# Sparse attention with residual and layer norm: three more output products in the last stretch, and additions moved behind the last tile

## The chip, the cores and the metric

The kernel runs on one core of a Trainium2 chip. The metric is device time in microseconds (us) of one execution, and the comparison is between medians of several executions. The engines are named as in the profile: PE (TensorE, with PEld for its weight loads), DVE (VectorE), ACT (ScalarE), POOL (GpSimd) and SP (SyncE, which here only issues DMAs).

## What is computed

There are 16 batches of 1024 nodes with 512 features, one 0/1 adjacency matrix for all of them, and 8 heads of 64. Each batch goes through masked attention, an output projection, the residual and a layer norm:

```python
q = (x @ Wq + bq).reshape(b, n, H, HD)
k = (x @ Wk + bk).reshape(b, n, H, HD)
v = (x @ Wv + bv).reshape(b, n, H, HD)
scores = jnp.einsum('bqhd,bkhd->bhqk', q, k) / jnp.sqrt(jnp.float32(HD))
scores = scores + (1.0 - adj)[None, None, :, :] * -1000000000.0
attn = jax.nn.softmax(scores, axis=-1)
out = jnp.einsum('bhqk,bkhd->bqhd', attn, v).reshape(b, n, d)
return out @ Wo + bo
# and around it:
x = _layernorm(x + _L0_gnn_ref(x, adj, ...), axis=-1)
```

The adjacency matrix is sparse: its first nodes have many neighbours and most have few.

## The kernel before

**Tiles.** The nodes are sorted by their number of neighbours, and the sorted order is cut into eight tiles of 128 queries. Tile `t` of batch `b` has the number `8 * b + t`. For a tile the kernel gathers one key and value row for each query and step, with an indirect DMA on POOL (L1260, tile `kvg`), so attention is a list of 530 steps, called *places*: a batch has 32 or 34 of them (batch 15, the last, has 34). A place multiplies queries and keys (DVE L1281), reduces by head (DVE L1285), exponentiates (ACT L1296), weighs the values (ACT L1309 or DVE L1313) and adds them up (DVE L1325, or PE L1334 and L1335 for steps whose rows belong to other tiles). When a tile is closed, `normalise` divides (DVE L1346 to L1355), PE transposes the result (L1369, `poT`), ACT copies it (L1373, `oT`).

**Fronts.** Beside attention, PE computes the projections of later batches (L748, L790 for q, L947 for keys and values in the seven-product form of Strassen). They are a list of units, `fronts`, worked off at a pace that is set at the start of each batch from what is left and from what the batch's own output products and sums will take. `fronts` is planned to be empty twelve places before batch 15 starts, 46 places before the end of attention. From there on is the last stretch.

**Output products.** `finish` multiplies a closed tile's `oT` by Wo on PE (L790, `po`). In the last stretch the bias is added by a small PE product (L1078), earlier by DVE. After attention's end `finish` adds the bias to y on DVE ahead of the product (L1067). `complete` then adds the residual y (DVE L1099 where the bias is added by DVE, and L1100), squares (ACT L1107), takes the power of the variance (POOL L1113, or L1143 for two tiles at once), shifts (DVE L1116), normalises (ACT L1121) and stores rows with an indirect DMA on POOL (L1125).

**The order of work.** The whole program is one loop over places, and each engine's instructions run in the order in which the loop emits them. `now[0]` is the place, `total` is 530. `later(k, fn)` puts a piece of work `k` places ahead (list `plan`), `later_last` puts it behind that place's weighing (list `rest`). Within a place come exponentials, products, gathers, weighing, adds, scores, then `normalise` of the tile closed one place before, then `plan`, then `rest`, then PE's units as far as a credit reaches. In the last stretch the credit grows by 3.4 a place (`LAST_SHARE`); an output product costs 4 x 0.86, about one place. No product may begin in the two places before the end:

```python
if (
    not finishing and len(done) > (LAZY if fronts else 0) and n > loaded.get(done[0], n) + 1
    and n > last_finish + bool(fronts) and not total - 2 <= n < total
):
```

**Spilled tiles.** Tiles whose number is in `SPILL` (20 of them: tiles 3 and 6 of batches 4 to 11, and 102, 103, 106, 107) aren't multiplied in their own batch. Their `oT` is written to DRAM by SP, and so is their x (`STORED`, tensor `residual`), two places before the x buffer is filled again. In the last stretch `reload` brings one of them back every second place: `oT` by SP (L1055, into the three buffers `e`, `w`, `g` that the fronts used) and y by SP (L1026) from `residual`, where a tile that isn't spilled has y gathered by POOL (L1029). PSUM tiles of these products rotate among four buffers with the tag `fill`.

Of the kernel before, what the change touches and what calls it, by code (L numbers as in the profile page):

```python
# [41 lines left out]

LAZY = 2

SPILL = (*(8 * b + t for b in range(4, 12) for t in (3, 6)), 102, 103, 106, 107)
STORED = {*SPILL, *(i for i in range(102, 128) if i % 8 > 1)}
LATE = 12

# [129 lines left out]
def kernel(  # L178
# [75 lines left out]
    with ExitStack() as main:  # L254
# [85 lines left out]
        def tiles_of(b):  # L340
            return [t for t in range(NT) if t or b < PAIRED_FROM or merged(b)]

        def number(b, t):
            return b * NT + t if t < NT else -1
# [3 lines left out]
        x_rows = x.rearrange("b n d -> (b n) d")  # L348
        spill = {i: dram.tile([P, D], F32, name=f"spill_{i}") for i in SPILL}
        residual = {i: dram.tile([P, D], F32, name=f"residual_{i}") for i in sorted(STORED)}  # L350
# [89 lines left out]
        now, plan, rest, urgent, known, waiting, combined = [0], {}, {}, [], [], [], []  # L440

        def later(k, fn):
            plan.setdefault(now[0] + k, []).append(fn)

        def later_last(k, fn):
            rest.setdefault(now[0] + k, []).append(fn)
# [337 lines left out]
        def product(name, lhs, w, out):  # L784

            def unit(c):
                if c == 0:
                    PS[name] = fill_psum(name)
                p = PS[name]
                nc.tensor.matmul(p, lhs(c), w[:, c, :], start=(c == 0), stop=(c == NPAIR - 1))  # L790
                if c == NPAIR - 1:
                    del PS[name]
                    later(1, lambda: out(p))

            return [(PRODUCT, lambda c=c: unit(c), None) for c in range(NPAIR)]
# [210 lines left out]
        def rows_of(b, t):  # L1006

            if t == LONE_TILE or t == 0 and merged(b):
                n, col, base = (2 * SPARED, NT + 2, b - 1) if t else (P, NT + 1, b - 1)
            elif t == MORE_TILE:  # L1010
                n, col, base = (LONE - SPARED) * (B - PAIRED_FROM), NT + 3, 0
            else:
                n, col, base = P, NT if t == ONE_KEY and b >= PAIRED_FROM else t, b
            return n, asked_row[0:n, col:col + 1], base * N * D
# [30 lines left out]
        def keep_mean(b, p):  # L1045

            m = work.tile([1, D], F32, tag="q", name=f"out_mean_{b}", bufs=2)
            nc.scalar.copy(m, p[0:1, :])
            nc.sync.dma_start(mean_rows[b:b + 1, :], m)
            if merged(b):  # L1050
                later(2, lambda: lone_tiles.append(b))
# [7 lines left out]
        def finish(b, t):  # L1059


            mean_row = t == ONE_KEY and b >= PAIRED_FROM
            plain = bool(fronts) or mean_row
            biased = not plain and now[0] < total

            if now[0] >= total and not plain:
                nc.vector.tensor_tensor(Y[b, t], Y[b, t], bo_bc, op=OP.add)  # L1067

            def out(p):
                OT.pop((b, t))  # L1070
                if mean_row:
                    keep_mean(b, p)
                complete(b, t, p, plain)

            units = product(f"po_{b}_{t}", lambda c: OT[b, t][:, ts(c, P)], W["o"], out)
            if biased:
                def bias():
                    nc.tensor.matmul(  # L1078
                        PS[f"po_{b}_{t}"], three.to_broadcast([P, P]), bo_3, start=False, stop=False
                    )  # L1080

                units.insert(2, (BIAS, bias, None))
            return units

        def complete(b, t, p, plain):
            n, rows, offset = rows_of(b, t)
            y, p = Y[b, t][0:n, :], p[0:n, :]
            single = fronts or now[0] > total + 3 or n < P
            if single:
                st = small.tile([P, 5], F32, name="stats", bufs=6)[0:n, :]  # L1090
            else:

                second = bool(half)
                if not second:
                    half.append([small.tile([P, 2, 5], F32, name="stats_2", bufs=5)])
                st2 = half[0][0]
                st = st2[:, int(second), :]
            if plain:
                nc.vector.tensor_tensor(y, p, y, op=OP.add)  # L1099
            nc.vector.scalar_tensor_tensor(  # L1100
                y, bo_bc[0:n, :] if plain else p, 1.0, y, op0=OP.mult, op1=OP.add, accum_out=st[:, 0:1]
            )

            def spread():

                sq = work.tile([P, D], F32, tag="ysq", name=f"ysq_{b}_{t}", bufs=1)
                nc.scalar.activation(sq[0:n, :], y, AF.Square, bias=st[:, 0:1], scale=-float(D), accum_out=st[:, 2:3])  # L1107

            def variance():
                nc.vector.tensor_scalar(st[:, 2:3], st[:, 2:3], 1.0 / D ** 3, EPS, op0=OP.mult, op1=OP.add)  # L1110

            def power():
                nc.gpsimd.tensor_tensor(st[:, 3:4], st[:, 2:3], neg_half[0:n, :], op=OP.pow)  # L1113

            def shift():
                nc.vector.scalar_tensor_tensor(  # L1116
                    st[:, 4:5], st[:, 0:1], -1.0 / D, st[:, 3:4], op0=OP.mult, op1=OP.mult
                )

            def norm_out():  # L1120
                nc.scalar.activation(y, y, AF.Identity, bias=st[:, 4:5], scale=st[:, 3:4])  # L1121
                later(2, store)

            def store():
                nc.gpsimd.indirect_dma_start(  # L1125
                    out=out_rows[b, t], out_offset=bass.IndirectOffsetOnAxis(ap=rows, axis=0),
                    in_=y, in_offset=None, element_offset=offset,
                )
                del Y[b, t]

            later_last(1, spread)
            if single:
                late = 1 if fronts else 0
                later(2 + late, variance)
                later(3 + late, power)
                later(4 + 2 * late, shift)
                later_last(5 + 2 * late, norm_out)
            elif second:
                later(3, variance)
                mate_shift, mate_norm_out = half.pop()[1]  # L1140

                def powers():
                    nc.gpsimd.tensor_tensor(  # L1143
                        st2[:, :, 3:4], st2[:, :, 2:3], neg_half[:, :, None].to_broadcast([P, 2, 1]), op=OP.pow
                    )

                def shifts():
                    mate_shift()
                    shift()

                later(4, powers)
                later(6, shifts)
                later_last(6, mate_norm_out)
                later_last(7, norm_out)
            else:
                later(3, variance)
                mine = half[0]
                mine.append((shift, norm_out))

                def alone():  # L1160
                    if half and half[0] is mine:
                        half.pop()
                        power()
                        later(2, shift)
                        later_last(3, norm_out)

                later(6, alone)
# [197 lines left out]
        def turn(b, t, o):  # L1365
            def transpose():
# [4 lines left out]
                def out():  # L1371
                    OT[b, t] = work.tile([P, D], F32, tag="oT", name=f"oT_{b}_{t}", bufs=LAZY + 2)
                    nc.scalar.copy(OT[b, t], p)  # L1373
                    if number(b, t) in SPILL:
                        later(1, lambda: nc.sync.dma_start(spill[b * NT + t], OT.pop((b, t))))
# [74 lines left out]
        done, coming, spilled, gathered, fronts, guarded = [], [], [], [0], [], []  # L1450

        total = len(blocks)

        def kept_y():
            return sum(t == "mean" or number(b, t) not in SPILL for b, t in Y)

# [24 lines left out]
        with tc.manual_schedule():  # L1481
# [9 lines left out]
            def needed(b, part):  # L1491
                b += int(part)
                if b >= B:
                    return fronts_time
                return fronts_by[b - 1] + (part - int(part)) * (fronts_by[b] - fronts_by[b - 1])
# [7 lines left out]
            while n < total or plan or rest or urgent or done or finishing or spilled or lone_tiles or not guarded:  # L1503
# [6 lines left out]
                elif n in start:  # L1510

                    b = start.index(n)
                    left = sum(u[0] for u in fronts)
                    ahead = EARLY + FIRST * (1 - max(0, b - 1) / LATE)
                    goal = fronts_time - needed(b + 2, ahead / NBT)
                    kept = sum(number(b, t) not in SPILL for t in tiles_of(b))
                    share = (max(0.0, left - goal) + kept * NPAIR * PRODUCT + NS * SUM) / (start[b + 1] - start[b])
# [105 lines left out]
```

## Time and profile before

| | |
|---|---|
| median of 5 runs | 1900.1 us (1887.47 to 1903.67) |
| the profiled execution, its own time | 1901.09 us |
| its span, first to last instruction | 1899.2 us |
| mean granted TensorE clock | 0.986 |
| spilled tiles brought back (`oTs<-spill`) | 20, issued from 1713.2 to 1846.2 us |
| indirect stores of rows (`out_dram<-y`, L1125) | 129 |
| gathers of y (L1029) on POOL, and loads of y by SP (L1026) | 93 and 36 |
| output products on PE (L790, `po`) | 816 records with `oT`, 160 with a reloaded `oTs` |

The profile is of one execution; its own time is 1.0 us above the median of the runs. Two records of L790 stand for one matmul of 128 x 128 by 128 x 512, so an output product has eight. Times of the timeline are us from the span's start. "[4.15 <-PE po L790]" behind an instruction says that its engine was idle for 4.15 us ahead of it, and who released it.

### The profile page before, as it was taken

To read this page: it belongs to the slowest core of one execution; us is meant where nothing else is said; L and a number is where in the kernel's file an instruction comes from. 1 tells how busy PE (TensorE), PEld (TensorE's weight loads), DVE (VectorE), ACT (ScalarE), POOL (GpSimd) and SP (SyncE) were. 2 spreads that over 40 slices of the span, in tenths; PEclk is the share of its full clock that TensorE was granted. 3 is DMA by queue.
4 is the path that set the end of the run, shared out by engine and by line. 5 is a ranking of instruction groups with operands and counts; after the bars stand their busy time and mean duration, and the time that the engine had idled before them with its cause. 6 is when DMAs were issued, how large, how long until landed. Compare 5 with 4: busy or idle time off the path is not lost.

```text
span 1899.2 us, 25241 instructions
## 1 busy us (share of the span) xinstructions
PE 1816.8 (96%) x5136; PEld 878.8 (46%) x5150; DVE 1687.1 (89%) x3462; ACT 1565.8 (82%) x6184; POOL 1268.6 (67%) x1189
## 2 busy tenths in 40 slices
PE   7969899999999999999999999999999999999995
PEld 3424444444444444444444445444444444444442
DVE  6878689999998999999899999999899999997784
ACT  3626768988888898999889898999799988987785
POOL 1355665776675777767676776777677776665783
PEclk9989999999999999999999999999999999999998
DMA  7355677898888889998898988998999999898992
GB/s 279 116 171 178 203 254 266 282 326 290 307 287 282 288 309 327 305 319 304 292 315 297 331 290 305 325 308 310 301 321 314 322 338 320 297 331 307 343 315 100
DMA packets 188150, 544.64 MB, mean 287 GB/s; under 512 B 32602, under 2 KB 32622, under 8 KB 187986
## 3 DMA queue, kind: packets, MB, share of 16 engines
q0 software_dynamic: 116400, 382.82, 61.0%
q1 hardware_dynamic: 68510, 154.30, 21.8%
q10 hardware_dynamic: 3076, 5.82, 0.9%
q14 instruction: 121, 0.99, 0.2%
q8 instruction: 43, 0.70, 0.1%
HBM read 419.52 MB, written 144.34 MB: 297 GB/s over the span
## 4 chain that ended last, share of the span: by engine, by line
PE 71%; DVE 12%; ACT 6%; issue 3%; DMA 2%; another core or an unknown queue 1%; POOL 1%; SPq 0%; DVEq 0%; POOLq 0%; ACTq 0%
PE po L790 18%; PE pq L790 14%; PE pp L947 12%; PE x L947 9%; PE z L947 9%; ACT pv L1309 3%; PE pxT L748 3%; PE poT L1369 2%; DVE qk L1281 2%; DVE s L1285 2%; PE sum L1335 2%; PE sum L1334 2%; DVE pv L1325 1%; ACT sq_k L800 1%
## 5 line engine op out<-in xcount | busy, mean ns | idle before, releaser
L1309 ACT ACTIVATE pv<-kvg,pv 128x64 f32<-128x64 f32 x3600 | 908.2, 342 | 2.2 <-issue 2.1
L1260 POOL DMA_INDIRECT kvg<-kv_pair,place_row x462 | 528.2, 1143 | 263.1 <-issue 89.4
L790 PE MATMUL po<-wo,oT 128*128 128x512 f32 x816 | 375.7, 598 | 0.9 <-ACT oT L1373 0.5
L790 PE MATMUL pq<-wq,xT 128*128 128x512 f32 x792 | 369.0, 597 | 2.9 <-DVE q L821 2.4
L1285 DVE TENSOR_REDUCE s<-qk 128x8 f32<-128x512 f32 x530 | 360.5, 680 | 6.7
L1281 DVE TENSOR_TENSOR qk<-qt,kvg 128x512 f32<-128x512 f32 x434 | 296.5, 683 | 0.8 <-DMA kvg<-kv_pair,place_row 0.8
L947 PE MATMUL x<-b,xT 128*128 128x512 f32 x504 | 238.8, 596 | 1.1 <-issue 1.0
L947 PE MATMUL pp<-t,s 128*128 128x512 f32 x504 | 237.2, 593 | 1.5 <-ACT sq_k L800 1.5
L790 PEld LDWEIGHTS po<-wo,oT 128*128 128x128 f32 x816 | 154.5, 192 | 177.0 <-issue 166.5
L1325 DVE TENSOR_TENSOR pv<-pv,pv 128x520 f32<-128x520 f32 x329 | 228.5, 694 | 4.0 <-ACT pv L1309 3.0
L790 PEld LDWEIGHTS pq<-wq,xT 128*128 128x128 f32 x792 | 148.0, 191 | 167.6 <-issue 153.8
L1001 POOL DMA_INDIRECT x<-in_x_dram,asked_row x120 | 132.0, 1100 | 77.0 <-PE pxT L748 32.0
L1125 POOL DMA_INDIRECT out_dram<-y,asked_row x129 | 147.2, 1141 | 40.7 <-issue 25.1
L1296 ACT ACTIVATE pv<-s,absent 128x8 f32<-128x8 f32 x434 | 127.2, 295 | 53.3 <-DVE s L1285 38.8
L800 ACT ACTIVATE sq_k<-kv 128x128 bf16<-128x128 f32 x512 | 151.0, 302 | 8.5 <-DVE kv L970 4.0
L947 PEld LDWEIGHTS x<-b,xT 128*128 128x128 f32 x504 | 94.8, 192 | 109.5 <-issue 103.2
L947 PEld LDWEIGHTS pp<-t,s 128*128 128x128 f32 x504 | 94.1, 190 | 109.3 <-issue 101.6
L1214 POOL DMA_INDIRECT qg<-q_rows,query_row x96 | 109.0, 1135 | 33.4 <-issue 25.9
L947 PE MATMUL z<-b,s 128*128 128x512 f32 x252 | 120.6, 601 | 4.7 <-DVE kv L975 4.4
L1029 POOL DMA_INDIRECT y<-in_x_dram,asked_row x93 | 100.3, 1078 | 36.0 <-issue 27.4
L947 PE MATMUL z<-t,s 128*128 128x512 f32 x252 | 119.6, 597 | 0.0
L947 PE MATMUL pp<-t,xT 128*128 128x512 f32 x252 | 118.5, 593 | 0.6 <-ACT oT L1373 0.6
(276 smaller groups left out, 2746.7 us busy)
## 6 DMA issues: line engine op xcount, KB each, us to landing
kv_pair<-kv SPq DMA_DIRECT2D x98, 512.0 KB
q_rows<-q SPq DMA_DIRECT2D x106, 256.0 KB
qt<-q_rows SPq DMA_DIRECT2D x98, 256.0 KB
residual<-x SPq DMA_DIRECT2D x36, 256.0 KB
y<-residual SPq DMA_DIRECT2D x36, 256.0 KB
kv_rows<-kv SPq DMA_DIRECT2D x15, 512.0 KB
kvg<-kv_pair,place_row POOLq DMA_INDIRECT x462
kv_pair<-kv SPq DMA_DIRECT2D x28, 256.0 KB
```

What stands on the lines that cost most here:

```text
L790: nc.tensor.matmul(p, lhs(c), w[:, c, :], start=(c == 0), stop=(c == NPAIR - 1))
L800: nc.scalar.activation(sq, s[:, ts(h, P)], AF.Square, scale=scale, accum_out=sums[:, h:h + 1])
L947: nc.tensor.matmul(R[bank], l[:, ts(c, P)], right[:, c, :], start=(first and c == 0), stop=(c == 1), skip_group_check=True,)
L1001: nc.gpsimd.indirect_dma_start(out=y, out_offset=None, in_=x_rows, in_offset=bass.IndirectOffsetOnAxis(ap=asked_row[:, t:t + 1], axis=0), ...
L1125: nc.gpsimd.indirect_dma_start(out=out_rows[b, t], out_offset=bass.IndirectOffsetOnAxis(ap=rows, axis=0), in_=y, in_offset=None, element_o ...
L1214: nc.gpsimd.indirect_dma_start(out=q, out_offset=None, in_=q_rows[b % ROWS], in_offset=bass.IndirectOffsetOnAxis(ap=rows, axis=0))
L1260: nc.gpsimd.indirect_dma_start(out=KG[n], out_offset=None, in_=rows, in_offset=bass.IndirectOffsetOnAxis(ap=(place_row if b else key_row)[ ...
L1281: nc.vector.tensor_tensor(QK[n], q, KG[n][:, 0:D], op=OP.mult)
L1285: nc.vector.tensor_reduce(S[n], QK.pop(n).rearrange("p (h d) -> p h d", d=HD), axis=AX.X, op=OP.add)
L1296: nc.scalar.activation(PV[n][:, D:], S.pop(n), AF.Exp, bias=bias)
L1309: nc.scalar.activation(pv[:, ts(h, HD)], v[:, ds(D + h * HD, HD)], AF.Copy, scale=pv[:, D + h:D + h + 1])
L1325: nc.vector.tensor_tensor(PV[b, t], PV[b, t], pv, op=OP.add)
```

## The change

Tiles 45, 69 and 93 (tile 5 of batches 5, 8 and 11) join the spilled ones, which are then 23. And where the last stretch is on and an output product's `out` comes up in one of attention's last three places (`total - 3` to `total - 1`), its `complete` is put off to place `total`. There it stands in `plan`, behind the last tile's `normalise`. The PSUM tile is held until then.

```diff
-SPILL = (*(8 * b + t for b in range(4, 12) for t in (3, 6)), 102, 103, 106, 107)
+SPILL = (*(8 * b + t for b in range(4, 12) for t in (3, 6)), 45, 69, 93, 102, 103, 106, 107)
 STORED = {*SPILL, *(i for i in range(102, 128) if i % 8 > 1)}
...
                 if mean_row:
                     keep_mean(b, p)
-                complete(b, t, p, plain)
+                if not fronts and total - 4 < now[0] < total:
+                    later(total - now[0], lambda: complete(b, t, p, plain))
+                else:
+                    complete(b, t, p, plain)
```

## The prediction

> **What bounds the kernel now.** I read the page first, then the windows of single batches, then the chain of waits inside two of them, and last the timeline of the final 45 us.
>
> ```profile
> span 1899.2 us, 25241 instructions
> PE 1816.8 (96%) x5136; PEld 878.8 (46%) x5150; DVE 1687.1 (89%) x3462; ACT 1565.8 (82%) x6184; POOL 1268.6 (67%) x1189
> PE 71%; DVE 12%; ACT 6%; issue 3%; DMA 2%; another core or an unknown queue 1%; POOL 1%; SPq 0%; DVEq 0%; POOLq 0%; ACTq 0%
> ```
>
> PE carries 71% of the chain that ended last, but 96% of busy PE is an average over unlike stages. So I cut the span at the first place of batches 5, 8, 11 and 13 (one L1285 reduction a place, counted off in the timeline) and added the last stretch, from the end of batch 14 until PE first runs dry. The columns are length, then busy time and count of PE, PEld, DVE, ACT, POOL, then granted clock, DMA share and GB/s.
>
> ```profile
> 728.50:833.20 104.70, 104.63 (x305) 51.38 (x305) 99.30 (x195) 95.85 (x397) 73.76 (x68) 1.00 0.93 313
> 1041.30:1143.20 101.90, 101.17 (x292) 49.52 (x291) 97.19 (x190) 91.71 (x369) 74.79 (x69) 1.00 0.93 316
> 1348.30:1451.90 103.60, 101.72 (x296) 49.63 (x296) 99.14 (x194) 94.02 (x391) 72.35 (x63) 1.00 0.90 310
> 1553.30:1649.00 95.70, 90.54 (x260) 44.16 (x260) 92.92 (x178) 88.29 (x374) 61.25 (x55) 0.98 0.91 315
> 1764.40:1861.60 97.20, 93.64 (x257) 44.22 (x260) 79.24 (x220) 76.69 (x245) 73.06 (x68) 0.98 0.89 311
> ```
>
> The first three rows are the batches that lose a product (tiles 45, 69 and 93 are tile 5 of batches 5, 8 and 11). PE is idle there for 0.07, 0.73 and 1.88 us; DVE is second, 3 to 5 us behind. In batch 13 DVE leads, and the time is 2.8 us above its 92.92. The chain, asked for batches 8 and 11 alone, says the same:
>
> ```profile
> by line: PE pq L790 21.9%; PE pp L947 21.0%; PE po L790 17.3%; PE x L947 13.5%; PE z L947 11.8%; PE pxT L748 4.7%; PE poT L1369 3.0%; PE sum L1335 2.6%; PE sum L1334 2.5%; PE pm L858 1.0%; DVE g L966 0.7%; issue 0.5%
> by line: PE po L790 19.8%; PE pq L790 16.5%; PE pp L947 14.8%; PE z L947 11.6%; PE x L947 8.3%; issue 3.3%; DVE qk L1281 2.9%; PE pxT L748 2.9%; PE poT L1369 2.7%; DVE s L1285 2.6%; ACT pv L1309 1.9%; PE sum L1335 1.7%; PE sum L1334 1.7%; D
> ```
>
> So a product removed from these batches should shorten them by about its PE time. The end looks different: after 1861.6 PE waits.
>
> ```profile
> 1861.60:1864.35 2.75, 0.00 (x0) 0.00 (x1) 2.68 (x9) 2.75 (x12) 0.00 (x0) 1.00 0.24 98
> 1864.35:1867.75 3.40, 0.66 (x4) 0.42 (x4) 3.40 (x11) 1.97 (x7) 3.05 (x3) 0.86 0.00 0
> 1867.75:1871.00 3.25, 3.22 (x6) 2.19 (x7) 1.46 (x6) 3.25 (x12) 1.47 (x3) 0.50 0.42 161
> 1880.10:1884.00 3.90, 3.90 (x5) 1.63 (x6) 1.03 (x4) 0.65 (x1) 2.56 (x3) 0.56 0.36 128
> ```
>
> PE has nothing to do for 2.75 us, then does 0.66 us in 3.40 while DVE is full, and then works at half clock. This is where products put off from the middle can go.
>
> **The change, part by part: what leaves the three batches.** The duration rows are three of the timeline and four groups of batch 8 (count, busy us, mean ns):
>
> ```profile
> 1842.31 1.88 PE L790 MATMUL po<-wo,oTs 128*128 128x512 f32 x4
> 1844.03 0.38 PE L1078 MATMUL po<-bo,three 128*128 128x512 bf16 x1
> 1845.96 0.59 PE L1334 MATMUL sum<-pv,sums 128*128 128x256 f32 x2
> L1099 DVE TENSOR_TENSOR y<-po,y 128x512 f32<-128x512 f32 x6 | 4.1, 681 | 0.0
> L1100 DVE SCALAR_TENSOR_TENSOR y<-bo_bc,y 128x512 f32<-128x512 f32 x6 | 4.2, 702 | 0.2
> L1107 ACT ACTIVATE ysq<-y,stats 128x512 f32<-128x512 f32 x5 | 3.6, 712 | 0.0
> L1121 ACT ACTIVATE y<-y,stats 128x512 f32<-128x512 f32 x6 | 4.8, 804 | 0.0
> L1125 POOL DMA_INDIRECT out_dram<-y,asked_row x7 | 7.5, 1072 | 2.0 <-issue 1.4 <-ACT oT L1373 0.3 <-ACT e L960 0.3
> ```
>
> From 1842.31 to 1845.96 PE does one biased product: 3.65 us. The row of four has (1.88 - 0.59) / 3 = 0.43 us from start to start; a product is eight such records, 3.44 us, so the bias is the other 0.21. In the middle a product has no bias row: each moved tile takes 3.44 us from PE there, 0.68 + 0.70 = 1.38 us from DVE, 0.71 + 0.80 = 1.5 us from ACT, and from POOL a store (1.07) and the gather of y. What comes in are two direct writes of 256 KB on SP's queue (oT to spill, x to residual); what goes out is a gather and a store of 256 KB each, so the batch's DMA bytes stay the same. SP's later transfers (the queries and the keys' rows) stand behind these writes, and the gather of the next x tile, which goes two places later, waits in POOL's queue until the residual write has left the buffer. Both have several places in hand; I take 0.7 us for all of it, between 0 and 5.1 us (3 x 512 KB at the 310 GB/s of batch 11).
>
> After the loss PE holds 101.2, 97.7 and 98.3 us in the three batches. DVE holds 97.9, 95.8 and 97.8; with batch 13's 2.8 us on top it reaches 100.7, 98.6 and 100.6. The later of the two is late next: 101.2, 98.6 and 100.6, which is 3.4 (PE's 3.44), 3.3 and 3.0 us less than now. That is 9.7 of the 10.3 us that leave PE; less the 0.7 I take **-9.0 us**. The lower end of the gain is 0 (second rival), the upper 13.3 (first rival).
>
> **Where the products go.** Count places from attention's end, so that -1 is the last of its 530. One spilled tile is loaded every second place, number k at place -46 + 2k. Before, number 19 is the last: loaded at -8, multiplied at -6, added at -5. Now number 20 is loaded at -6 and multiplied at -4; number 21, loaded at -4, falls due at -2, where no product may begin, and goes to 0; number 22 goes to +1. Of the natural tiles, (15, 7) is multiplied at -3 and (15, 6), the last, is transposed at +1 and multiplied at +3. The additions due at -3 (number 20) and at -2 (tile (15, 7)) now stand at place 0, behind the last tile's normalising. Those due at -5 and before are untouched. The rows of the end as it is:
>
> ```profile
> 1869.65 3.62 PE L790 MATMUL po<-wo,oT 128*128 128x512 f32 x4
> 1871.03 2.01 ACT L1309 ACTIVATE pv<-kvg,pv 128x64 f32<-128x64 f32 x8
> 1873.49 1.94 PE L790 MATMUL po<-wo,oT 128*128 128x512 f32 x4
> 1875.46 0.69 DVE L1100 SCALAR_TENSOR_TENSOR y<-po,y 128x512 f32<-128x512 f32 x1 [4.15 <-PE po L790]
> 1876.08 0.70 DVE L1325 TENSOR_TENSOR pv<-pv,pv 128x520 f32<-128x520 f32 x1
> 1877.72 0.69 DVE L1355 TENSOR_TENSOR o<-o,rden 128x512 f32<-128x512 f32 x1
> 1878.46 0.66 PE L1369 MATMUL poT<-ident,o 128*128 128x128 f32 x4 [3.04 <-DVE o L1355]
> 1880.09 5.40 PE L790 MATMUL po<-wo,oT 128*128 128x512 f32 x8 [0.19 <-ACT oT L1373]
> 1885.52 0.69 DVE L1100 SCALAR_TENSOR_TENSOR y<-po,y 128x512 f32<-128x512 f32 x1 [4.32 <-PE po L790]
> 1888.18 1.04 POOL L1125 DMA_INDIRECT out_dram<-y,asked_row  x1 [0.20 <-issue]
> 1889.52 0.96 POOL L1125 DMA_INDIRECT out_dram<-y,asked_row  x1 [0.30 <-issue]
> ```
>
> *The wait that goes.* DVE stands 4.15 us for the product of (15, 7), with the last tile's last add (1876.08) queued behind. That add needs only ACT's weighing, which ends at 1873.04. Without the addition in front it runs 3.0 us earlier, and the last tile's o is ready at 1878.4 - 3.0 = 1875.4.
>
> *What PE does instead.* Number 20 starts behind the transposes at 1865.0 and ends at 1868.65; the sums (0.9) follow to 1869.6, (15, 7) with bias to 1873.25 (now at full clock), number 21 without bias to 1876.7. Only then comes the last transpose, until 1877.4; number 22 ends at 1880.85, with oT's copy under it, and the last product at 1884.4, against 1885.5 before. It counts 3.44 us and not the 5.40 of the row at clock 0.56, since PE has not been idle ahead of it. So PE takes three more products and still ends 1.1 us sooner: they fill 2.8 us of idleness, the lost half clock, and the wait of 3.0 us ahead of 1878.46.
>
> The Trainium skill ("TensorE: Matmul & The Clock Gate", Part 1) says that the clock halves after an idle window of about 3.4 us and that the windows run freely. By that, the gap at 1861.6 may still cost half a window, an estimated 1.7 us more at the end; the trace has both outcomes (1.00 in the gap, 0.50 soon after), so it does not fix which.
>
> *What is late next.* Stores. The shifts of the two put-off tiles stand at place +6, those of 21 and 22 at +8, all behind the last tile's addition (+4) on DVE; their normalising lies on ACT behind the last tile's squares, and their stores on POOL ahead of the last store. Before, one store (1888.18) stood there. From one store to the next POOL takes 1.34 us (1889.52 - 1888.18), so five instead of two add 3 x 1.34 = 4.0 us. **Tail: -1.1 + 4.0 = +2.9 us.** If the stores hid, it would be -1.1; the far end is the third rival.
>
> *Cover of the loads.* The three reloads must land before PE comes to them.
>
> ```profile
> 1846.16 0.32 SPq L1055 DMA_DIRECT2D oTs<-spill  x1
> 1846.52 11.04 SPq L1026 DMA_DIRECT2D y<-residual  x3
> 1757.74 12.34 DMA oTs<-spill
> 1771.28 3.62 PE L790 MATMUL po<-wo,oTs 128*128 128x512 f32 x4 [3.12 <-issue]
> ```
>
> Number 22 reuses the buffer of number 19, which PE leaves at 1861.6. Even with the longest landing that the chain shows, 12.34 us, it is there at 1873.9; PE wants it at 1877.4. Nothing is charged.
>
> **Sum.** -9.0 + 2.9 = -6.1 us against the profiled execution's 1901.09 us: 1895.0. That execution lay 1.0 us above the median of 1900.1, so the forecast for a median is 1894 us.
>
> **Rivals.** *A tile is worth more than its product.* Batch 3 spills nothing, batch 7 two tiles:
>
> ```profile
> 513.60:628.90 115.30, 111.92 (x317) 54.17 (x317) 101.32 (x200) 99.24 (x405) 74.91 (x71) 0.99 0.86 282
> 939.30:1041.30 102.00, 100.93 (x293) 48.98 (x293) 97.93 (x192) 92.79 (x386) 68.29 (x65) 1.00 0.89 304
> ```
>
> Of 24 PE records less, 16 are those two products; 13.3 us x 16/24 / 2 = 4.4 us a tile, because idle time went with it. Three tiles give -13.3, with the tail -10.4: 1890 us for a median. Against it: batches 5 and 8 have no such idle time left.
>
> *PE does not pace the middle.* DVE is at 95% and might be the true pace, coupled through the hand-written order. Then the middle gives nothing and the tail stays: 1903 us. For it: batch 13. Against it: the chain of batch 8, where PE holds nearly every step. The Trainium skill ("Trainium Kernel Development and Optimization", Performance Expectations) calls matmul busy time a bad metric and weight loads the good one; by it, with 49.52 of 101.90 us loading, PE would have room and this rival would hold. The trace speaks against that here: its starts lie 0.43 us apart without a gap.
>
> *Slower: the last reloads come late.* One late reload stopped PE for 3.12 us, and the half clock behind the stop cost 3.62 - 1.88 = 1.74 more. Three such stops at 20, 21 and 22 add 14.6 us to the last tile's path: -6.1 + 14.6 = +8.5, 1909 us. It decides once a load takes over 15 us from the release of its buffer. SP's wait in the 11.04 us row speaks for it, the low DMA share after 1861 (0.24, 0.00) against.
>
> **How the numbers follow.** The forecast case gets 0.45, the first rival 0.27, PE not pacing 0.11, late reloads 0.17. Half a per cent, 9.5 us, is about what a measurement of this kernel can tell from no change. Faster than that are the first rival and a third of the forecast case's spread (a tail cheaper by 3): 0.27 + 0.15 = 0.42. Slower than that is half of the last rival, whose centre is +8.5 (0.09), and a third of the second, with the writes at their 5.1 and the half-clock 1.74 on top of the tail (0.04): 0.13. The rest is 0.45. The range, 1885 to 1906, runs from the first rival with a tail at -1.1 (-14.4) to the second with half of the writes' 5.1 (+5.4).
>
> **What the new profile would show.** Right: PE busy 3 to 4 us less in each of batches 5, 8 and 11 and these shorter by the same; 23 reloads; DVE's add L1325 no longer behind a wait for L790; PE nearly full between 1865 and the end; five stores in a row on POOL behind the last addition. Wrong: batches as long as before with DVE at 97% or more; PE stopped ahead of an oTs product in the last 20 us; the last product again at half clock.

## The result and the profile after

The change moved the time by less than a measurement can tell. The median is 1891.46 us (44 runs) against 1892.67 us for the kernel before (86 runs); the ratio is 0.9993 with a 95% interval from 0.9982 to 1.0003, which is -1.3 us, from -3.4 to +0.6. The forecast was 1894 us and -6.1 us; -6.1 lies outside the interval. The profiled execution of the changed kernel spans 1883.0 us, 16 us less than the one of before. Single executions spread that far (1884 to 1912 us before, 1880 to 1905 us after), and most of the difference lies ahead of place 0 of batch 2, where the two programs do the same. So I compare stages, not spans.

The page of the changed kernel, span and busy time:

```profile
span 1883.0 us, 25251 instructions
PE 1808.9 (96%) x5137; PEld 876.0 (47%) x5151; DVE 1688.0 (90%) x3461; ACT 1565.0 (83%) x6184; POOL 1265.4 (67%) x1184
```

PE has about the same number of records as before (products moved, none was dropped). The windows of batches 5, 8 and 11, as before in the order length, PE, PEld, DVE, ACT, POOL, clock, DMA share, GB/s:

```profile
715.10:815.70 100.60, 100.38 (x292) 49.12 (x292) 97.76 (x190) 95.97 (x401) 73.28 (x66) 1.00 0.93 323
1023.10:1125.40 102.30, 99.31 (x281) 48.60 (x280) 96.03 (x186) 88.96 (x361) 72.83 (x67) 0.97 0.92 316
1329.20:1433.30 104.10, 103.33 (x302) 50.86 (x302) 98.37 (x190) 93.90 (x391) 70.37 (x65) 1.00 0.92 322
```

Batch 5 is 4.1 us shorter, where 3.4 was forecast; PE has 13 records less there, the product's eight and five others. Batch 8 isn't shorter: PE has 11 records less, but is idle for 3.0 us and runs part of the time at half clock (0.97). In batch 11 other front units moved in, so PE has 6 records more than before.

The end came nearly as worked out. The windows from PE's first stop on:

```profile
1842.16:1844.90 2.74, 0.00 (x0) 0.00 (x1) 2.67 (x9) 2.74 (x12) 0.00 (x0) 0.88 0.84 277
1844.90:1848.00 3.10, 3.10 (x7) 1.84 (x8) 3.10 (x10) 1.67 (x6) 2.75 (x3) 0.56 0.26 94
1848.00:1861.70 13.70, 13.70 (x39) 6.67 (x38) 8.31 (x30) 11.18 (x31) 7.48 (x8) 1.00 0.34 127
```

The timeline's rows of the last tile (its last add, its transpose, its product, its addition) and of the last five stores:

```profile
1853.62 0.70 DVE L1328 TENSOR_TENSOR pv<-pv,pv 128x520 f32<-128x520 f32 x1 [1.75 <-ACT pv L1312]
1858.33 0.60 PE L1372 MATMUL poT<-ident,o 128*128 128x128 f32 x4
1862.31 3.60 PE L790 MATMUL po<-wo,oT 128*128 128x512 f32 x8
1865.95 0.69 DVE L1103 SCALAR_TENSOR_TENSOR y<-po,y 128x512 f32<-128x512 f32 x1 [1.52 <-PE po L790]
1868.55 1.04 POOL L1128 DMA_INDIRECT out_dram<-y,asked_row  x1 [0.17 <-issue]
1869.89 0.96 POOL L1128 DMA_INDIRECT out_dram<-y,asked_row  x1 [0.30 <-ACT y L1124]
1871.16 0.96 POOL L1128 DMA_INDIRECT out_dram<-y,asked_row  x1 [0.30 <-ACT y L1124]
1872.42 0.96 POOL L1128 DMA_INDIRECT out_dram<-y,asked_row  x1 [0.31 <-ACTq L1596]
1873.69 0.96 POOL L1128 DMA_INDIRECT out_dram<-y,asked_row  x1 [0.30 <-issue]
```

The last add now waits only for ACT's weighing; PE is full from 1844.90 to the last product; the last product runs at full clock (3.60 us where it took 5.40); and five stores follow each other behind the last addition. From PE's first stop to the end of the span it was 37.6 us (1899.2 - 1861.6) and is 40.8 us (1883.0 - 1842.16): +3.2, where the forecast had +2.9. What is missing is the gain in the middle.

### The profile page after: what moved, and what is told of

Same layout as the page of the kernel before. It is cut to its first block, busy times and chain, and to the rows that moved or that the text cites. A ratio compares the mean times of both kernels' runs of the same rounds, so it can differ in the third digit from the quotient of the medians.

```text
span 1883.0 us, 25251 instructions
## 1 busy us (share of the span) xinstructions
PE 1808.9 (96%) x5137; PEld 876.0 (47%) x5151; DVE 1688.0 (90%) x3461; ACT 1565.0 (83%) x6184; POOL 1265.4 (67%) x1184
## 5 line engine op out<-in xcount | busy, mean ns | idle before, releaser
L790 PE MATMUL po<-wo,oT 128*128 128x512 f32 x792 | 361.0, 593 | 0.4 <-ACT oT L1376 0.3
L790 PEld LDWEIGHTS po<-wo,oT 128*128 128x128 f32 x792 | 148.7, 190 | 168.5 <-issue 161.2
L1128 POOL DMA_INDIRECT out_dram<-y,asked_row x129 | 146.3, 1134 | 39.9 <-issue 25.7
```

What stands on the lines that cost most here:

```text
L1128: nc.gpsimd.indirect_dma_start(out=out_rows[b, t], out_offset=bass.IndirectOffsetOnAxis(ap=rows, axis=0), in_=y, in_offset=None, element_o ...
```

## Experiments

All kernels were timed in turns with the kernel before on the same chip; twelve runs in three sessions, each on another chip, in which the kernel before had medians of 1881.95, 1891.93 and 1862.75 us. "The first stop" is PE's stop of 2.7 us behind the product of place -6; it is a mark by which the ends of the traces can be laid over each other.

### The two parts, each alone

```diff
# e1: after, without the putting off        # e2: before, with it
-if not fronts and total - 4 < now[0] < total: ...     +if not fronts and total - 4 < now[0] < total: ...
 SPILL = (..., 45, 69, 93, 102, 103, 106, 107)          SPILL = (..., 102, 103, 106, 107)
```

> The three tiles are spilled, no addition is put off. The batches are those of the changed kernel, so all that differs from it is the end. Theory P (the prediction's terms): the batches give -9.0 us in all. Theory Q (batch 8 meets a new stop of PE of 3 us ahead of the front product z, and half clock behind it, since the removed output product was what PE did while DVE combined x; it comes back in every execution): the stop at z is there again in batch 8 and the batches give only -3 to -4.5. Both expect of the end that the two additions at -3 and -2 delay the last tile's add by about 1 us, which PE's queue hides, and that their shifts come ahead of the last tile's addition, so that 3 stores and not 5 stand behind it: end +0.2 against before, 2.7 us better than with the put-off additions.

> No tile more is spilled; only the addition of tile (15, 7) at place -2 goes behind the last tile's normalising. All theories: the batches are as before within the spread of single executions; the last tile's last add comes 3.0 us sooner after the last weighing, PE is still idle ahead of the last transpose, and the end is 2.4 to 4.2 us shorter, by how much of the last product runs at half clock. Against that, no gain would say that the 4.15 us wait was not on the path.

Spilling alone gave 0.9978 (0.9959 to 0.9997), -4.1 us. Its end isn't the +0.2 that I expected: from the first stop to the end of the span it takes 41.0 us, as long as with the additions put off. The last add comes 13.9 us behind the first stop, and POOL still issues its last five stores from 26.0 us behind it on, with the last tile's power ahead of four of them. So with 23 spilled tiles the second half of the change is worth 0.2 us at the end; the times of the two, -4.1 and -1.3 us, don't differ by more than their intervals.

Putting off alone gave 0.9991 (0.9973 to 1.0010), -1.7 us, too little for the timing to show. Its end shows in the trace: 35.5 us against 37.6, -2.1 us, with the last add at 11.5 us from the first stop and not at 14.5. The wait was on the path. The expected 2.4 to 4.2 us was a little too much. PE is no longer idle ahead of the last transpose, and the last product ran at full clock, so that the last addition starts 20.6 us behind the first stop and not 23.9. But 1.2 of these 3.3 us are lost again behind it:

```profile
1853.97 3.70 PE L790 MATMUL po<-wo,oT 128*128 128x512 f32 x8 [0.95 <-ACT oT L1376]
1861.52 1.04 POOL L1128 DMA_INDIRECT out_dram<-y,asked_row  x1 [1.38 <-ACT y L1124]
```

The first of the last two stores comes 3.8 us behind the start of the last addition (1857.71), where it was 2.7 before (1888.18 and 1885.52): the put-off tile's normalising on ACT now stands behind the last tile's squares.

### The middle alone

```diff
# e3: SPILL with 45, 69, 93; they are spilled and never brought back
-                        spilled.append((b, t))
+                        if number(b, t) not in (45, 69, 93):
+                            spilled.append((b, t))
```

> Leaves out the output of tiles 45, 69 and 93: they are spilled in their batches as in the change, and never brought back, multiplied, added or stored; no addition is put off. The end is that of before, so the time against before is the worth of the three products in the middle by itself. Theory P: -9.0 us. Theory Q: -3 to -4.5 us, with the stop ahead of z in batch 8. Theory R (PE does not pace the middle): 0 within 2 us.

It gave 0.9969 (0.9953 to 0.9985), -5.8 us, from -8.8 to -2.8. The prediction's -9.0 lies just outside of that, and theory R is out. Single traces don't fix the size. From the first place of batch 4 to that of batch 12 it is 822.8 us with the additions put off alone, and 812.5, 814.1 and 813.3 us in the session's three runs without these tiles (spilling alone, this run, the later last addition), on average 9.5 us less and so about what was forecast. Between the profiles of the kernel before and the changed one, it is 823.0 and 820.1 us. The stop in batch 8 was there in this run, in the spill-only run and in the run below with a later last addition (2.95 to 3.3 us), so it belongs to the program. Rows of the changed kernel, of spilling alone, and of tile 77 in its place:

```profile
1087.32 3.78 PE L947 MATMUL z<-b,s 128*128 128x512 f32 x4 [2.98 <-DVE kv L975]
```

```profile
1087.78 1.99 PE L947 MATMUL z<-b,s 128*128 128x512 f32 x4 [3.02 <-DVE kv L975]
```

```profile
1077.21 1.02 PE L858 MATMUL pm<-vsum,mean 128*1 128x512 f32 x2 [2.22 <-DVE vsum L854]
```

In the first two PE comes to the second z product while DVE still combines the next x tiles (L774 to L777, ahead of L975 on its queue): the units between the two z products (one, where it was two and a place more) no longer cover it. This looked like the whole loss, so I tested it.

### Another tile than 69

```diff
-SPILL = (..., 45, 69, 93, 102, 103, 106, 107)
+SPILL = (..., 45, 77, 93, 102, 103, 106, 107)
```

> The changed kernel with tile 77 (batch 9) spilled in place of 69 (batch 8); the end is the same program. With 77 the two z products of batch 10's first pair lie in places 283 and 285 again as before, with the transposes between them; with 69 they lie in 285 and 286, one unit apart. Theory Q (the stop of 3 us and the half clock behind it are made by tile 69's removal): no stop ahead of z in batch 8, no new one of over 1.5 us in batch 9, the middle gives -9, the end +3.2 as in the changed kernel, in all -6 us against before (0.997). Theory P' (a moved tile is worth 2 us wherever it comes from): -2.6 us (0.9986), as with 69.

> Leaves out the output of tiles 45, 77 and 93, as the run with 45, 69 and 93 left out did (that gave 0.9969): spilled and never brought back. The end is that of before. Theory Q: without the stop in batch 8 the three tiles give their full 9 to 10 us (0.995). Theory P': again -5.8 us (0.9969).

With 77 the stop at z in batch 8 was gone, and the time was no better: 0.9987 (0.9966 to 1.0009) for the whole change, -2.5 us, and 0.9968 (0.9947 to 0.9989) for the middle alone, -6.1 us. Another stop stands in its place in both runs, the 2.22 us in the third row above (a third run with 77, further down, doesn't have it). The two times are those of theory P', but theory Q's 0.997 and 0.995 lie inside the intervals too (and so does -9.0 us for the middle), so these runs lean against Q and don't decide. Two runs further down do: the one with two tiles, and the one with PE's work cut, where PE never stops for over 1.6 us in these batches and much of the cut is lost all the same. The stop is real, but it isn't the whole loss.

### Two tiles instead of three

```diff
+SPILL = (..., 45, 93, 102, 103, 106, 107)
```

> The changed kernel with tiles 45 and 93 alone spilled in addition (22 in all). Theory Q: the middle gives -6 to -6.5, without a stop in batch 8; of the last reloads only one product comes after attention's end, so that 4 stores instead of 5 stand at the end: end +1.9 against before; in all -4.5 us (0.9976). Theory P': middle -4, in all -2 us (0.9989).

1.0003 (0.9982 to 1.0024), +0.6 us. Both expectations missed its centre; that of P' (0.9989) lies in the interval, that of Q (0.9976) outside, though PE has no stop over 1.5 us in batches 4 to 11. Its end took 40.3 us from the first stop, with the last product at 5.39 us (half clock again), so 2.7 us were lost there and not 1.9.

### How much PE's time is worth

Four runs take away or add one cost each, over all of batches 4 to 11, so that the effect is larger than the spread.

```diff
# e9: eight output products issue one of four matmuls (tile 5)
+                if name not in THIN:
                     nc.tensor.matmul(p, lhs(c), w[:, c, :], start=(c == 0), stop=(c == NPAIR - 1))
+                elif c == 0:
+                    nc.tensor.matmul(p, lhs(c), w[:, c, :], start=True, stop=True)
# e10: 36 additions on DVE left out
-            if plain:
+            if plain and not (4 <= b < 12 and t not in (ONE_KEY, LONE_TILE)):
                 nc.vector.tensor_tensor(y, p, y, op=OP.add)
# e11: as e3, for tile 5 of batches 4 to 11
# e12: the writes of a spill for those tiles, which are multiplied in place all the same
-                    if b * NT + t in STORED:
+                    if b * NT + t in STORED | EXTRA:
                         nc.sync.dma_start(residual[b * NT + t], xs)
...
+                        if number(b, t) in EXTRA:
+                            later(1, lambda: nc.sync.dma_start(spill[b * NT + t], OT[b, t]))
```

> The kernel before, with PE's work alone cut: the output product of tile 5 of batches 4 to 11 issues one of its four matmuls (so these eight tiles' output lacks three quarters of the product); the planner still counts four, so the order of all else is the same. PE loses 8 x 6 records x 0.43 = 20.6 us in the batches. Theory P (PE paces the batches alone): -19 to -21 us (0.989 to 0.990). Theory H1 (PE paces part of the time, another engine or the DMA the rest; a microsecond less on PE is worth half): -9 to -13 us (0.9935 to 0.995). Theory H2 (the product is worth all of its PE time, but a spill's own writes and the later load of x eat 1.2 us a tile): -19 to -21.

> The kernel before, with DVE's work alone cut: of the tiles of batches 4 to 11 that are multiplied in the middle (36 of them, without the one-key and the lone tiles) the addition of the residual (L1099) is left out, so their output lacks the product. DVE loses 36 x 0.61 = 22 us, about what the run with PE's work cut loses on PE. Theory P and H2: DVE is hidden, 0 to -3 us. Theory H1: DVE paces the rest of the time, -6 to -11 us (0.994 to 0.997).

> As the runs with three tiles left out, with tile 5 of all eight batches 4 to 11: spilled and never brought back, its output left out. Theory P: 8 x 3.0 = -24 us (0.987). Theory H1 and H2, by the -6 us that three tiles gave: -16 us (0.9915).

> The kernel before, with the spill's own cost added and nothing taken away: tile 5 of batches 4 to 11 has its x and its oT written to DRAM and the next x loaded two places later, as a spilled tile has, and is multiplied in its batch all the same. Theory H2: +8 to +12 us (1.004 to 1.006). Theory P and H1: 0 to +3 us; the bytes, 8 x 512 KB, are 13.5 us of DMA time at 310 GB/s if none of it is hidden.

| run | taken away or added, batches 4 to 11 | ratio (95%) | us |
|---|---|---|---|
| PE's work cut | PE 20.6 us | 0.9937 (0.9924 to 0.9951) | -11.7 |
| DVE's work cut | DVE 22 us | 1.0001 (0.9993 to 1.0010) | +0.2 |
| eight tiles left out | PE 27.5 us, and all else of them | 0.9909 (0.9893 to 0.9924) | -17.0 |
| a spill's writes added | 8 x 512 KB, later loads of x | 0.9999 (0.9991 to 1.0008) | -0.2 |

A microsecond less on PE is worth 11.7 / 20.6 = 0.57 us (0.44 to 0.69); with whole tiles 17.0 / 27.5 = 0.62 us (0.52 to 0.72). A spill's writes cost nothing that the timing shows, so theory H2 falls. DVE's work by itself doesn't either, so half of theory H1 falls: PE paces these batches, but relieving it doesn't pay in full. Part of the reason shows in the windows of batches 4 to 11, first with the writes added, then with PE's work cut, then with DVE's cut, then with eight tiles left out:

```profile
607.60:1422.60 815.00, 813.94 (x2354) 398.74 (x2353) 779.73 (x1526) 742.10 (x3022) 589.54 (x535) 1.00 0.91 317
```

```profile
607.00:1412.60 805.60, 797.88 (x2312) 390.27 (x2311) 778.56 (x1525) 741.50 (x3022) 592.02 (x535) 1.00 0.91 316
```

```profile
609.50:1424.40 814.90, 812.62 (x2352) 398.71 (x2351) 757.49 (x1491) 740.32 (x3016) 592.18 (x535) 1.00 0.90 312
```

```profile
607.90:1409.20 801.30, 791.16 (x2291) 388.11 (x2290) 767.68 (x1487) 730.56 (x2998) 566.48 (x511) 1.00 0.92 317
```

With nothing taken away PE is idle for 1.1 us in 815.0. With 20.6 us cut its busy time falls by 16.1 us, and it is idle for 7.7 us: the stretch is 9.4 us shorter. These are one execution each; in the profile of the kernel before PE is idle for 7.3 us of 823.0, also with nothing taken away, so this pair alone doesn't prove the reading that follows. What PE waits for, from the waits of these two windows, first with the writes added, then the longest four of nine with PE's work cut:

```profile
PE pm L859 <- DVE vsum L855: 0.4, 1, 0.4
PE po L791 <- ACT oT L1374: 0.3, 1, 0.3
PE pxT L749 <- DVE q L822: 0.2, 1, 0.2
```

```profile
PE pxT L749 <- DVE q L825: 2.8, 2, 1.6
PE pq L792 <- DVE q L825: 1.1, 1, 1.1
PE pxT L749 <- DVE y L1103: 1.1, 1, 1.1
PE pm L862 <- DVE vsum L858: 0.4, 1, 0.4
```

As these rows have it, a product removed lets PE run ahead until it meets an operand, or a PSUM tile, that DVE or ACT hasn't released yet. The 4.5 us between 20.6 and 16.1 are for the most part work that moved in: the output products lost all of their 48 records (360 of tile `po` are 312, and 142.5 us where it was 163.1), but the window holds only 42 records less, since four of z and two of x of later front products, some 3.0 us, now fall into it. Without them the stretch would be shorter by an estimated 12 us, near the 11.7 us of the timing. In the window with eight tiles left out PE also ran at half clock twice, for 3.4 us each (0.50 from 1071.0 and from 1265.6 us), so not all of that run's loss is waiting. DVE's cut gave nothing while PE was full; whether less work on DVE would pay once PE's work is cut, when most of PE's waits are for DVE, wasn't tested, nor was ACT's.

### The end in another order

```diff
# e4: after, and the last tile's addition eight places later
+                elif (b, t) == (B - 1, 6):
+                    later(8, lambda: complete(b, t, p, plain))
# e8: SPILL with 45, 77, 93; two places later; every tile's power by itself from place 0 on
+                elif (b, t) == (B - 1, 6):
+                    later(2, lambda: complete(b, t, p, plain))
-            single = fronts or now[0] > total + 3 or n < P
+            single = fronts or now[0] >= total or n < P
```

> The changed kernel with the last tile's addition written eight places later, behind the shifts, normalising and stores of the four tiles that were queued behind it. If the pile of five stores is what lengthens the end (+4.0 us of the +2.9), the last addition starts no later in time, one store is left behind it (two at most), and the end is 3 to 4 us shorter than the changed kernel's. If the end is bound by PE's three more products, nothing changes.

> As with tile 77, and the end written in another order: each tile that is added after attention's end takes its power alone, and the last tile's addition stands two places later, so that the others' shifts and normalising come ahead of it on DVE and ACT, and its power ahead of the last two stores on POOL. If POOL's queue of stores and powers bounds the end, the time from PE's first stop to the end falls from 40.9 to 36 to 37 us; the whole is 4 us less than with tile 77 alone: -10 us against before by theory Q (0.995), -7 by P'. If it is PE that bounds the end, it stays at 40.9.

Eight places later gave 0.9987 (0.9971 to 1.0004), -2.4 us; its end takes 39.9 us, like that with tile 77 (39.7), which has no half clock in it either. So it gained nothing. The row that explains it is the last tile's power, which now stands on POOL behind the stores; its input was ready at 1857.27, when DVE's L1115 had ended:

```profile
1858.70 0.96 POOL L1130 DMA_INDIRECT out_dram<-y,asked_row  x1 [0.31 <-issue]
1859.69 0.58 POOL L1118 TENSOR_TENSOR stats<-stats,neg_half 128x1 f32<-128x1 f32 x1
1861.64 1.04 POOL L1130 DMA_INDIRECT out_dram<-y,asked_row  x1 [1.38 <-ACT y L1126]
```

Two places later, with single powers, gave 0.9971 (0.9952 to 0.9989), -5.5 us against before: with spilling alone the second version here, with nothing left out, whose interval lies below that of no change, though its distance to the same tiles in the old order (0.9987) isn't settled by the timing. Its end takes 38.6 us, 1.1 less than 39.7; I had expected 36 to 37. The last rows of POOL:

```profile
1884.97 0.96 POOL L1130 DMA_INDIRECT out_dram<-y,asked_row  x1 [0.31 <-issue]
1885.96 0.57 POOL L1118 TENSOR_TENSOR stats<-stats,neg_half 128x1 f32<-128x1 f32 x1
1886.72 1.04 POOL L1130 DMA_INDIRECT out_dram<-y,asked_row  x1 [0.19 <-issue]
1888.07 0.96 POOL L1130 DMA_INDIRECT out_dram<-y,asked_row  x1 [0.30 <-issue]
```

The last tile's power follows a store without a gap, and another store (1886.72) still goes ahead of the last one. In both runs the power waits for stores while its input is there (for 2.4 and 1.8 us), so POOL's queue bounds these two ends; the order that would take all of it away wasn't found.

## Why the prediction was right or wrong

**What bounds the kernel: right, but not in the way it was used.** PE paces the middle: cutting DVE by as much gives nothing. But the step "a product removed from these batches should shorten them by about its PE time" failed. The prediction read the chains of batches 8 and 11 as saying the same; that of batch 11 had issue (3.3%), DVE L1281 and L1285 (2.9% and 2.6%) and ACT L1309 (1.9%) in it.

**The middle, -9.0 us: the term that was mis-sized.** Three tiles gave -5.8 and -6.1 us in two runs, 2.0 us a tile and not 3.0; the run with eight gives 2.1 (1.8 to 2.5), which shuts 3.0 out. The failing step is "the later of the two is late next": it took the later of PE's and DVE's busy time, with batch 13's 2.8 us as all that the coupling costs, and found 9.7 of 10.3 us visible. Measured over batches 4 to 11, on the chip of that session, 57 to 62% are visible. Sums of busy time bound a stretch from below; they don't say when two engines at 100% and 95% will meet. With 0.6 the middle comes to -6.2 us. What makes up the lost 40% is shown only in part: waits for DVE and ACT, half clock in some runs, and for the rest it stays open.

**The 0.7 us for the writes: too much.** By it eight tiles would have cost 1.9 us; their writes cost -0.2 us (-1.7 to +1.5).

**Where the products go and what PE does instead: right.** With tile 77, where the clock didn't halve, the last product ended 22.6 us behind the first stop; the working had 1884.4 - 1861.6 = 22.8. The last add came 3.0 us sooner, as said. In the changed kernel itself the last product ended only 0.1 us sooner than before (23.75 us behind the first stop, 23.88 before) and not 1.1.

**Stores: right.** Five stand at the end, 1.26 to 1.34 us apart; they add 3.8 us, where 4.0 was worked out.

**The end, +2.9 us: right in sum, and in part by luck.** The 1.0 us that PE's part came short by was offset in part by stores 0.2 us cheaper and by 0.4 us less behind the last store (9.3 us from its start to the end of the span, 9.7 before), which the working didn't have. The profiled +3.2 includes a half-clock window at the first stop (0.88 and 0.56 in the first two windows of the end), which I had left to the Trainium skill's sentence ("TensorE: Matmul & The Clock Gate", Part 1) with an estimated 1.7 us. The end with tile 77 has none and takes 1.1 us less, so the same gap can go either way: a stop of 2.74 us was enough in the changed kernel, less than the 3.4 us that the sentence has, and one of 2.75 us wasn't with tile 77.

**The putting off.** I never priced it by itself within the change. It is worth 2.1 us without the three tiles and 0.2 us with them: PE's queue, not DVE's wait, then sets the last transpose.

**The rivals.** A tile worth more than its product: out, it is worth less. PE not pacing: out in the form that I gave it; a rival between ("PE paces, and 40% comes back") was missing. The Trainium skill's rule on busy time and weight loads ("Trainium Kernel Development and Optimization", Performance Expectations) is about how close a kernel is to roofline; I had read it as giving PE room at 49% weight loads. The runs speak against that reading: of the two cuts, PE's shortened the time and DVE's didn't. Late reloads: none at the end.

**The sum.** -6.2 and +3.2 make -3.0 us; measured were -1.3 (-3.4 to +0.6). The sign that was forecast isn't settled, and the result lies within half a per cent, the likeliest of the three cases. That 1894 us came within 2.5 us of the median is luck, as the kernel before lay 7.4 us lower than the median that the forecast started from.

## What to carry to other kernels

In a stretch where one engine is full and the next at 95%, a microsecond taken from the first can be worth well under a microsecond: here 0.6, and a cut over eight batches measured that at once where the change itself couldn't. Price a move of work at both ends: the place that receives it pays with its queues, here five stores in order on POOL with a small operation of the last tile behind them. And lay traces over each other by a mark in the program, since single executions of one program lay 20 us apart while the stretch from that mark to the end repeated within about two.

## What the runs showed of the hardware that I hadn't expected

The same stop of PE, 3.0 us long, was followed by no half clock in the spill-only run, by 3.4 us of it with the tiles left out, and by 6.8 us in the changed kernel, where the four matmul records behind it took 3.78 us instead of 1.99. And the kernel before differed by 1.6% between sessions (1862.75 to 1891.93 us in the medians), with a spread of 8 us in the fastest session and 16 to 19 us in the others.
